# A convolution, attention and expert kernel: a new start of the first image, and a new order where the second attention begins

## The chip, the cores and the metric

The kernel runs on one core of a Trainium2 chip. The metric is the time of one launch on the device in microseconds, the median of several runs. One further execution was recorded by the hardware profiler; its trace gives every instruction with its start, its duration and what it waited for. The engines are TensorE (PE in the profile, with its weight loads as PEld), VectorE (DVE), ScalarE (ACT), GpSimd (POOL) and SyncE (SP), which issues most of the transfers (DMAs). "Granted clock" is the share of TensorE's full clock that the chip's throttle allows.

## The reference

Two images of 256 channels and 56 x 56 pixels pass through two layers, all in float32:

```
x = x + conv_attn(group_norm(x))         # layer 0
t = tokens(x)                            # 6272 tokens of 256 features
t = t + linear_attention(layer_norm(t))  # layer 1
t = t + experts(layer_norm(t))
out = image(t)
```

conv_attn: a 1x1 convolution from 256 to 768 channels, a 3x3 convolution of each channel by itself, and attention of 8 heads over 7 x 7 neighbourhoods. Four heads (split 0) look at direct neighbours, four (split 1) at every second pixel. Scores get a bias from a table by relative position, softmax, the weighted sum of the values, and a projection. group_norm takes mean and variance over groups of 8 channels and all pixels:

```
m = mean(v over 8 channels, h, w);  s = var(...);  (v - m) / sqrt(s + eps)
```

linear_attention: with Q = elu(q) + 1 and K = elu(k) + 1 the sums K'V and K'1 over all tokens of an image, the message Q(K'V) / (Q K'1), a projection, a layer norm, a feed-forward layer of 512 units on token and message, and a second layer norm with weight g2 and bias b2. experts: a router picks the best 2 of 8 experts for each token; each expert is a layer norm, 256 -> 1024, gelu, 1024 -> 256, with bias b2 of its own; the two results are weighed by the softmax of the two logits.

## The kernel before

The program is written in one pass, and a scheduler places each engine's instructions by its own estimate of when their inputs are ready, unless `manual_schedule` keeps the written order of the engines that it names (PE in most of the kernel). `issue_after(x)` puts the instructions of its block behind x on x's engine; `high_priority` moves them forward. Each engine takes its instructions in the order so fixed.

Stages in order of time:

- **First image, 0 to about 430 us.** `Convolutions` loads image 0 into `x_sb` ([128, 2, 3136]: two halves `ct` of 128 channels), and `norm_image` counts it in groups of 448 pixels (`bn_stats`, L478), combines (L480), averages over groups of channels by a product with `g8` (L486, L492), takes the power -1/2 on POOL (L151) and scales `x_sb` in place (L499). `run` then goes over 6 blocks of 128 output channels and over two halves of the image: four groups of rows (8, 8, 8 and 5) get the 1x1 convolution, two products each (L529: one for each ct, each two instructions of PE), ACT copies them into the padded `ypad` (L535), and the 3x3 convolution follows: 8 rows on PE by nine products with diagonal weights (L550), the rest by nine DVE operations (L579) after a first one on ACT (L569). Attention of image 0 is interleaved, its PSUM tiles being `s_ps` (four banks, scores) and `po` (two banks, values and sums). `bias_tables` prepares the tables exp(bias) in the meantime: a frame of zeros `pf` goes to DRAM (L371), the turned biases into it (L374, L379), it comes back (L383), ACT takes the exponential (L387), POOL masks it (L405 to L409), and `fetch` loads the tables `tab` (L714). `wpr` (L639) holds the projection's weights.
- **Linear attention, first half of the tokens, 430 to 747.** Keys (`keys`: statistics, xt L155, K'V L317, running sum L324), then a pipeline over six groups of four token blocks: `queries`, `message`, `feed_forward`, `route`. The remaining convolutions of image 1 fill gaps. b2 is added to the tokens by POOL in `message` (L1925); in the second half and for the block that both halves share it is added in `keys` (L300). `route` has four parts: logits (L2052); the two best (L2084 and the `top_two` chain on DVE); places in the experts' lists (pp, L2099 and L2100, from the partial sums L2095) and `weights` with an exponential on ACT (L2037); and the scatter of the rows into `xs` by POOL (L168), with two stores of the tokens into y2 by ACT (L2000).
- **Second attention, image 1, 747 to 1043.** `Attention.run` is a generator; each of its yields is a step, counted by i. The steps of the first blocks turn 112 x 128 blocks to channels first (`prepare`, `turned`: four transposes on PE, L767; `settle`: copies to qT0, qT1, kT0, kT1 by ACT and DVE, L776 to L792), for which two PSUM banks take turns. A step of scores has four products (L652), the exponential (L656) and the multiply by the table (L657, DVE); a step of values has the products L666. At the steps of `ENDING` the routing of the last two groups of the first half is finished, and from step `LEAD` on every step of scores or values also runs one step of the experts.
- **Experts.** `fetch` loads the 256 rows `xr` of a tile (L1544, behind the scatters) and the expert's weights `w1e` (L1548) and `w2e` (L1552); `turn` transposes xr (L1584), scales it to `xe` (L1587), and `weigh` compares the rows' expert number and makes the weights (`eq` L1572, `idi` L1574, L1575, L1576; DVE); then 8 x 2 products (L1617), gelu (L1621) and 2 x 8 products (L1637) follow. In the second attention, tiles 0 and up run in this way.
- **Linear attention, second half, with experts, 1043 to 1424; experts alone to 1962; output to 1984.**

Of the kernel before, what the change touches and what calls it, by code (L numbers as in the profile page):

```python
# [62 lines left out]
NFI = 14  # L63
LEAD = 22
FILLS = (0, 2, 12, 18, 24, 27, 33)
# [61 lines left out]
def hybrid_kernel(ctx: ExitStack, tc: tile.TileContext, a: dict, out: bass.AP):  # L127
# [139 lines left out]
    def keys(tk, wk, sm, ps, bank, w_k, b2, kx, acc, n0, n, p, first, last, eager):  # L267
# [27 lines left out]
        for k in range(n):  # L295
            nc.scalar.activation(
                t[:, k, :], t[:, k, :], AF.Identity, bias=up[:, 1, k : k + 1], scale=up[:, 0, k : k + 1]
            )
        if b2 is not None:
            nc.gpsimd.tensor_tensor(t, t, b2[p].unsqueeze(1).to_broadcast([rows, n, C]), ALU.add)  # L300
        yield
# [61 lines left out]
    def bias_tables(sp, ac, pp):  # L363

        held = []
        for s in range(2):
            pf = sp.tile([NH * 21, 33], F32, name=f"pf{s}", bufs=1)
            nc.vector.memset(pf, 0.0)
            rpb = a[f"L0_conv_rpb{s}"]
            frame = dram.tile([NH, 21, 33], F32, name=f"frame{s}")  # L370
            nc.sync.dma_start(frame.rearrange("h r c -> (h r) c"), pf)  # L371
            turned = dram.tile([NH * 13, 13], F32, name=f"turned{s}")
            with nc.allow_non_contiguous_dma(reason="676 values"):
                nc.sync.dma_start(  # L374
                    turned, bass.AP(rpb.tensor, rpb.offset + 12, [[13, NH * 13], [-1, 13], [1, 1]])
                )
            held.append((pf, frame, turned))
# [7 lines left out]
        for s in range(2):  # L385
            nw, pf = wide[s], held[s][0]
            nc.scalar.activation(pf, pf, AF.Exp)  # L387
            far = sp.tile([NH * 21, 2], F32, name=f"far{s}", bufs=1)
            nc.sync.dma_start(far, a["c_far"])

# [9 lines left out]
            )  # L400
            nc.sync.dma_start(cm, a[f"c_cm{s}k"].rearrange("p (c j) -> p c j", j=nw))
            o = 0
# [16 lines left out]
    class Convolutions:  # L419


        def __init__(self, ctx):
            pool = lambda name, bufs, **kw: ctx.enter_context(tc.tile_pool(name=name, bufs=bufs, **kw))
            self.xp = pool("p1x", 1, side="right")
            self.cw = pool("p1w", 1, side="right")
            self.yp = pool("p1y", 2, side="right")
            self.sp = pool("p1s", 2, side="right")
            self.banks = [pool("p1pc", 1, space=PSUM, side="right")]
            self.turns = 0
            self.dp = None  # L430

            self.x_sb = self.xp.tile([P, 2, T], F32, name="x_sb")
            self.ypads = [self.cw.tile([P, HH // 2 + 2, WW + 2], F32, name=f"ypad{hf}") for hf in range(2)]
            for hf in range(2):
                nc.gpsimd.memset(self.ypads[hf][:, hf * (HH // 2 + 1), :], 0.0)
                nc.gpsimd.memset(self.ypads[hf][:, :, 0:1], 0.0)
                nc.gpsimd.memset(self.ypads[hf][:, :, WW + 1 : WW + 2], 0.0)
            self.load_x(0)
            self.g8 = self.cw.tile([P, P], F32, name="g8")
            nc.scalar.dma_start(self.g8, a["c_g8"])  # L440
            self.w2 = self.cw.tile([P, 6, 9], F32, name="w2")
            nc.scalar.dma_start(
                self.w2, a["L0_conv_w_qkv2"].rearrange("(oc p) one kh kw -> p oc (one kh kw)", p=P)
            )
            self.wq1 = self.cw.tile([P, 2, 3 * C], F32, name="wq1")
            nc.sync.dma_start(self.wq1, a["w_qkv1_t"].rearrange("(ct p) o -> p ct o", p=P))

# [55 lines left out]

        def run(self):


            w2 = self.w2
            for _ in self.norm_image():
                pass
            yield 0, 0  # L510
            for b, oc in ((b, oc) for b in range(B) for oc in range(6)):
                diag = None
                for hf in range(2):
# [10 lines left out]
                    ypad = self.ypads[hf]  # L524
                    q0 = r0 - hf
                    for g0, n in ((0, 8), (8, 8), (16, 8), (24, 5)):
                        py = self.bank([P, 8, WW], "py")
                        for ct in range(2):
                            nc.tensor.matmul(  # L529
                                py[:, :n, :], self.wq1[:, ct, oc * P : (oc + 1) * P],  # L530
                                self.x_sb[:, ct, (q0 + g0) * WW : (q0 + g0 + n) * WW],
                                start=(ct == 0), stop=(ct == 1),
                            )
                        k0 = 1 - hf + g0
# [72 lines left out]
    class Attention:  # L607
# [6 lines left out]
        def __init__(self, ctx, b, order, banks=None, spare=None):  # L614
# [10 lines left out]
            self.wpr = op.tile([P, 2, C], F32, name="wpr", bufs=1)  # L625
            if not banks:
                self.load_projection()
            self.ones = op.tile([TT, HD], F32, name="ones2", bufs=1)
# [12 lines left out]
        def scores(self, nk, parts, table, nj):  # L641
# [14 lines left out]
            nc.scalar.activation(p[:nk, :, :n], s_ps[:nk, :, :n], AF.Exp)  # L656
            nc.vector.tensor_tensor(grid(p), grid(p), table[:nk], ALU.mult)  # L657
            return grid(p)
# [65 lines left out]
        def run(self):  # L724
# [47 lines left out]
            def settle(g, k, pm):  # L772
# [7 lines left out]
                else:  # L780
                    one = pm[:, :G].rearrange("p (r pi c pj) -> p pi pj r c", pi=2, pj=2, c=28)
                    for pi in range(2):
# [7 lines left out]
                        else:  # L790
                            for pj in range(2):
                                (nc.scalar.copy if banks and g < 2 else evac)(  # L792
                                    kT1[:, pi, pj, :, r0 : r0 + 4, :],
                                    one[:, pi, pj].rearrange("p r (cc c) -> p cc r c", c=KC),
                                )

            def prepare(g):
# [266 lines left out]
    def first_image(conv, ph):  # L1064
# [4 lines left out]
        conv.share(ctx)  # L1069
        run, steps = conv.run(), att.run()  # L1070
        need = next(steps)
        tables = bias_tables(conv.sp, att.pool["ac"], att.pool["p"])
        next(tables)
        for k, (b, done) in enumerate(run):
            if k == 5:
                with tc.issue_after(anchors["copied"]):
                    next(tables, None)
# [277 lines left out]
    class Experts:  # L1355
# [222 lines left out]
        def turn(self, x, pools):  # L1578
# [12 lines left out]
            if x.eq is None:  # L1591
                self.weigh(x)
            b2 = pools.b2e()
# [65 lines left out]
    def linear(ph, tk, half, behind=None):  # L1659
# [258 lines left out]
        def message(n0, n, qz, out):  # L1918
# [3 lines left out]
            for k0 in range(0, n, 2):  # L1922
                if half == 0:
                    tt = tk.at(n0 + k0, 2)
                    nc.gpsimd.tensor_tensor(tt, tt, b2.unsqueeze(1).to_broadcast([P, 2, C]), ALU.add)  # L1925
                pm = ps_h.tile([P, 2, C], F32, name="pm", tag="h")
# [26 lines left out]
        def feed_forward(n0, n, m2T, out):  # L1953
# [15 lines left out]
            for k0 in range(0, n, 2):  # L1969
# [24 lines left out]
                yield  # L1994

        def store(n0, n):

            for k0 in range(0, n, 2):
                kn = min(2, n - k0)
                ins = nc.scalar.dma_start(  # L2000
                    y2[(n0 + k0) * P : (n0 + k0 + kn) * P, :].rearrange("(n p) c -> p n c", p=P),
                    tk.at(n0 + k0, kn),
                )
                if (n0, n) in order[early1:]:
# [28 lines left out]
        def weights(rt, ms, row, n):  # L2033

            r = rt.sm.tile([P, 4], F32, name="rsum")[:, :n]
            with tc.issue_after(newest[3]) if half and newest[3] is not None else nullcontext():
                nc.scalar.activation(ms[1], ms[1], AF.Exp)  # L2037
# [95 lines left out]
        def all_keys():  # L2133
# [6 lines left out]
            for i in range(len(pairs) + 2):  # L2140
                for k in (1, 0, 2):
                    j = i - k
                    if j == i and j < len(pairs):
                        live[j] = keys(
                            tk, wk, sm, ps_a, bank, w_k, b2 if half or pairs[j][1] == 1 else None, kx, acc, *pairs[j], j == 0, j == len(pairs) - 1, j < 3 and half == 0
                        )
# [327 lines left out]
```

## Time and profile before

| | |
|---|---|
| median of three runs | 1997.98 us (1995.13 to 2001.15) |
| profiled execution | 1985.54 us, its span 1983.8 us |
| PE busy | 1840.1 us (93%) |
| DVE, ACT, POOL busy | 1093.3, 705.8, 578.8 us |
| first product of the 1x1 convolution | 18.49 us from the start |
| mean granted clock | 0.972; 0.51 from 750 to 775, 0.67 from 775 to 800 |

A row of a timeline is: start, duration, engine, line, operation, output<-inputs, shape, count, and in brackets how long the engine stood idle before it and what ended that. "ACTq" and "SPq" are the queues of those engines issuing a DMA. A stretch's row gives the busy time of each engine with the number of instructions in brackets, the granted clock, the DMA engines' share and GB/s.

### The profile page before, as it was taken

To read this page: it belongs to the slowest core of one execution; us is meant where nothing else is said; L and a number is where in the kernel's file an instruction comes from. 1 tells how busy PE (TensorE), PEld (TensorE's weight loads), DVE (VectorE), ACT (ScalarE), POOL (GpSimd) and SP (SyncE) were. 2 spreads that over 40 slices of the span, in tenths; PEclk is the share of its full clock that TensorE was granted. 3 is DMA by queue.
4 is the path that set the end of the run, shared out by engine and by line. 5 is a ranking of instruction groups with operands and counts; after the bars stand their busy time and mean duration, and the time that the engine had idled before them with its cause. 6 is when DMAs were issued, how large, how long until landed. Compare 5 with 4: busy or idle time off the path is not lost.

```text
span 1983.8 us, 27692 instructions
## 1 busy us (share of the span) xinstructions
PE 1840.1 (93%) x9996; PEld 1304.7 (66%) x9996; DVE 1093.3 (55%) x2728; ACT 705.8 (36%) x1337; POOL 578.8 (29%) x634
## 2 busy tenths in 40 slices
PE   6999899988989997999989989999999999999996
PEld 3444454556645564665668755668788888888885
DVE  6887988889888546555557434655622222222121
ACT  2233324334434223544536543323322222222332
POOL 4520042025202444111126311345422323222221
PEclk9999999999989996999999999999999999999998
DMA  4644422350003334754464210114677676767995
GB/s 113 152 114 128 152 75 84 101 151 35 25 33 94 107 85 140 205 153 137 130 191 126 72 35 32 46 62 133 182 227 198 185 201 186 200 190 197 299 279 166
DMA packets 200147, 268.79 MB, mean 135 GB/s; under 512 B 30952, under 2 KB 158614, under 8 KB 199760
## 3 DMA queue, kind: packets, MB, share of 16 engines
q1 hardware_dynamic: 167920, 223.95, 37.4%
q0 software_dynamic: 19728, 27.54, 7.4%
q10 hardware_dynamic: 12352, 15.43, 2.3%
q8 instruction: 81, 1.33, 0.3%
q14 instruction: 66, 0.54, 0.1%
HBM read 200.19 MB, written 70.95 MB: 137 GB/s over the span
## 4 chain that ended last, share of the span: by engine, by line
PE 48%; DMA 5%; DVE 3%; ACT 3%; issue 1%; SPq 0%; POOL 0%; ACTq 0%; DVEq 0%; POOLq 0%
PE ph L1617 13%; PE py L1637 13%; PE p L1961 4%; DMA xr<-xs 2%; PE x L1637 2%; PE py L1977 2%; PE x L1617 2%; DMA xs<-in_c_fill 2%; PE po L666 2%; PE pm L1931 1%; PE kx L317 1%; PE x L359 1%; PE kp L305 1%; PE pq L1888 1%; PE px L1584 1%; PE s_ps L652 1%
## 5 line engine op out<-in xcount | busy, mean ns | idle before, releaser
L1617 PE MATMUL ph<-xe,w1e 128*128 128x256 f32 (+1 forms) x1448 | 309.2, 369 | 10.6 <-ACT hT L1621 4.1
L1637 PE MATMUL py<-w2e,hT 128*128 128x256 f32 x1392 | 311.3, 379 | 0.0
L1621 ACT ACTIVATE hT<-ph,sv 128x256 f32<-128x256 f32 (+1 forms) x362 | 165.7, 462 | 387.3 <-PE ph L1617 384.2
L1617 PEld LDWEIGHTS ph<-xe,w1e 128*128 128x128 f32 x1448 | 261.2, 190 | 49.8 <-ACT hT L1621 6.1
L1637 PEld LDWEIGHTS py<-w2e,hT 128*128 128x128 f32 x1392 | 260.1, 190 | 33.1 <-issue 0.2
L168 POOL DMA_INDIRECT y<-yt,idi x101 | 160.2, 1587 | 322.6 <-DVE yt L1643 178.2
L579 DVE SCALAR_TENSOR_TENSOR yc<-ypad,w,yc 128x1120 f32<-128x1120 f32 x144 | 202.5, 1410 | 31.4 <-ACT yc L569 29.0
L262 POOL TENSOR_TENSOR rs<-rs,mhalf 128x2 f32<-128x2 f32 (+3 forms) x90 | 72.8, 812 | 325.4 <-DVE rs L261 277.6
L529 PE MATMUL py<-x_sb,wq 128*128 128x448 f32 (+1 forms) x384 | 155.9, 538 | 8.3 <-ACT ypad L535 4.4
L656 ACT ACTIVATE p<-s_ps 112x952 f32<-112x952 f32 (+5 forms) x88 | 102.1, 1160 | 150.6 <-PE s_ps L652 101.4
L1574 DVE CAST idi<-xr 128x2 int32<-128x2 f32 (+1 forms) x53 | 10.9, 205 | 255.9 <-DMA xr<-xs 255.9
L657 DVE TENSOR_TENSOR p<-p,tab 112x952 f32<-112x952 f32 (+5 forms) x88 | 122.0, 1389 | 47.4 <-ACT p L656 47.3
L550 PE MATMUL pc<-ypad,diag 128*128 128x448 f32 x324 | 131.4, 547 | 0.0
L1643 DVE SCALAR_TENSOR_TENSOR yt<-py,eq,yt 128x256 f32<-128x256 f32 x87 | 41.7, 482 | 156.3 <-PE py L1637 156.1
L1599 POOL TENSOR_SCALAR yt<-b2e,eq 128x256 f32<-128x256 f32 x101 | 50.7, 507 | 257.6 <-DMA b2e<-in_L_ffn_b 198.6
L529 PEld LDWEIGHTS py<-x_sb,wq 128*128 128x128 f32 x384 | 72.2, 199 | 71.4 <-issue 55.7
L168 POOL DMA_INDIRECT xs<-row,si x98 | 97.5, 995 | 64.4 <-DVE si L2108 34.7
L572 DVE SCALAR_TENSOR_TENSOR yc<-ypad,w,yc 128x784 f32<-128x784 f32 x96 | 104.9, 1114 | 1.3 <-ACT yc L569 0.9
L666 PE MATMUL po<-p,v 98*32 98x170 f32 (+5 forms) x960 | 70.8, 376 | 28.6 <-DVE p L657 15.3
L550 PEld LDWEIGHTS pc<-ypad,diag 128*128 128x128 f32 x324 | 60.0, 191 | 52.3 <-issue 48.5
L1961 PE MATMUL p<-xT,fw 128*128 128x512 f32 (+1 forms) x208 | 93.6, 573 | 0.0
L1961 PE MATMUL p<-m2T,fw 128*128 128x512 f32 (+2 forms) x224 | 93.4, 539 | 0.0
(394 smaller groups left out, 2883.8 us busy)
## 6 DMA issues: line engine op xcount, KB each, us to landing
w1e<-in_L_ffn_W SPq DMA_DIRECT2D x53, 1024.0 KB
w2e<-in_L_ffn_W SPq DMA_DIRECT2D x53, 1024.0 KB
yd<-yc SPq DMA_DIRECT2D x24, 784.0 KB
ld<-yd SPq DMA_DIRECT2D x28, 448.0 KB
xr<-xs SPq DMA_DIRECT2D x48, 260.0 KB
b2e<-in_L_ffn_b SPq DMA_DIRECT2D x53, 128.0 KB
t<-td SPq DMA_DIRECT2D x12, 512.0 KB
y<-t ACTq DMA_DIRECT2D x24, 256.0 KB
```

The costliest lines, as they stand in the source:

```text
L168: ins = nc.gpsimd.indirect_dma_start(out=dst[:, :], out_offset=bass.IndirectOffsetOnAxis(ap=index, axis=0), in_=src, in_offset=None, **kw,)
L529: nc.tensor.matmul(py[:, :n, :], self.wq1[:, ct, oc * P : (oc + 1) * P], self.x_sb[:, ct, (q0 + g0) * WW : (q0 + g0 + n) * WW], start=(ct ...
L550: nc.tensor.matmul(pc, diag[:, tap, :], ypad[:, dy : dy + SHARE, dx : dx + WW], start=(tap == 0), stop=(tap == 8),)
L572: nc.vector.scalar_tensor_tensor(yc[:, y0:y1, :], src, w, yc[:, y0:y1, :], ALU.mult, ALU.add)
L579: nc.vector.scalar_tensor_tensor(yc[:, y0:y1, :], src, w, yc[:, y0:y1, :], ALU.mult, ALU.add)
L656: nc.scalar.activation(p[:nk, :, :n], s_ps[:nk, :, :n], AF.Exp)
L657: nc.vector.tensor_tensor(grid(p), grid(p), table[:nk], ALU.mult)
L666: nc.tensor.matmul(dst[hs] if w is None else den[hs], v[:nk, hs] if w is None else w[:nk, :], p[:, h, :, o : o + q.shape[2]], start=first ...
L1617: nc.tensor.matmul(p1, x.w1[:, ct, j * P : (j + 1) * P], x.xe[:, ct, :], start=(ct == 0), stop=(ct == 1),)
L1621: newest[3] = nc.scalar.activation(hT[:, j, :], p1, AF.Gelu, bias=x.sv[:, 4 + j : 5 + j]).ins
L1637: nc.tensor.matmul(py, hT[:, j, h * P : (h + 1) * P], x.w2[:, j, :], start=(j == 0), stop=(j == NJ - 1),)
L1961: nc.tensor.matmul(p1[:, :w], fw1[:, k, oc * P : (oc + 1) * P], rhs, start=(k == 0), stop=(k == 3))
```

## The change

1. **Head.** The loads of x go half by half over both queues, with g8 and the first 128 columns of the weights between; a new `first_block`, with PE and DVE in the written order, counts and scales half 0 while half 1 loads, and starts six row groups' products with half 0. The six places are the attention's s_ps and po banks; half 1's products complete them, and `run` takes them from `self.ready`. The clearing of pf, the small loads of `bias_tables` and image 0's wpr are put behind DVE's second count of half 1 or behind the first frame's store.
2. **b2.** It is always added in `keys`; the addition in `message` is gone.
3. **Stores and exponentials.** The exponentials in `weights` and the token stores that are written after the first block's last copy (`settled`) are put behind that copy on ACT. This concerns the last two groups of the first half.
4. **Rows compared.** `weigh`, called from `turn`, is put behind the latest multiply by a table on DVE.
5. **Experts two steps later.** LEAD is 24 instead of 22.

```diff
-LEAD = 22
+LEAD = 24
@@ keys
-        if b2 is not None:
-            nc.gpsimd.tensor_tensor(t, t, b2[p]..., ALU.add)
+        nc.gpsimd.tensor_tensor(t, t, b2[p]..., ALU.add)
@@ message
-                if half == 0:
-                    tt = tk.at(n0 + k0, 2)
-                    nc.gpsimd.tensor_tensor(tt, tt, b2..., ALU.add)
@@ bias_tables
-            nc.vector.memset(pf, 0.0)
+            with tc.issue_after(anchors["counted"]), tc.high_priority():
+                nc.vector.memset(pf, 0.0)
...
-            nc.sync.dma_start(frame.rearrange("h r c -> (h r) c"), pf)
+            ld = nc.sync.dma_start(frame.rearrange("h r c -> (h r) c"), pf)
+            anchors.setdefault("framed", ld.ins)
# the loads of turned, far and cm, and image 0's load_projection():
+            with tc.issue_after(anchors["framed"]), ...
@@ Convolutions
-            self.load_x(0)
+            for ct in range(2):
+                for k, (c0, c1) in enumerate(zip((0, G, 3 * G, 5 * G), (G, 3 * G, 5 * G, T))):
+                    eng = nc.scalar if k % 2 else nc.sync
+                    eng.dma_start(self.x_sb[:, ct, c0:c1], xv[0, :, ct, c0:c1])
+                if ct == 0:
+                    nc.scalar.dma_start(self.g8, a["c_g8"])
+                    nc.sync.dma_start(self.wq1[:, :, :P], wq1[:, :, :P])
...
-            nc.sync.dma_start(self.wq1, a["w_qkv1_t"]...)
+            nc.scalar.dma_start(self.wq1[:, :, P:], wq1[:, :, P:])
@@ first_block (new; count, mean, variance, scaled and products are small helpers)
+            with tc.manual_schedule(engines={PE, DVE}):
+                count(0, *range(NG))
+                mean(0)
+                variance(0)
+                count(1, 0)
+                scaled(0, 0, G)
+                products(0, 0)
+                count(1, 1)
+                scaled(0, G, T // 2)
+                products(0, 1)
+                count(1, *range(2, NG))
+                mean(1)
+                scaled(0, T // 2, T)
+                products(0, 2)
+                variance(1)
+                products(0, 3, 4, 5)
+                scaled(1, 0, G)
+                products(1, 0)
+                scaled(1, G, T // 2)
+                products(1, 1, 2)
+                scaled(1, T // 2, T)
+                products(1, 3, 4, 5)
+            self.ready = {r[:2]: d for r, d in zip(rows, places)}
@@ Convolutions.run
+                        py = self.ready.pop((hf, g0), None)
+                        if py is None:
+                            py = self.bank([P, 8, WW], "py")
+                            for ct in range(2):
+                                self.product(py, oc, hf, g0, n, ct)
@@ scores
-            nc.vector.tensor_tensor(grid(p), grid(p), table[:nk], ALU.mult)
+            anchors["scaled"] = nc.vector.tensor_tensor(...).ins
@@ settle, k == 3
+                                if banks and g == 0:
+                                    anchors["settled"] = ins.ins
@@ Experts.turn
-                self.weigh(x)
+                with tc.issue_after(anchors["scaled"]):
+                    self.weigh(x)
@@ linear
+        def behind():
+            turned = run == 0 and half == 0 and "settled" in anchors
+            return tc.issue_after(anchors["settled"]) if turned else nullcontext()
# in store: with behind(): the DMA; in weights, first half: with behind(): the exponential
```

## The prediction

> **What bounds the kernel now.** First the page's head, then the chain of waits, then busy time by stretches, and last the timelines of single engines where TensorE (PE) stands still. Engine shares and granted clock by fortieths of the span (49.6 us each):
>
> ```profile
> PE 1840.1 (93%) x9996; PEld 1304.7 (66%) x9996; DVE 1093.3 (55%) x2728; ACT 705.8 (36%) x1337; POOL 578.8 (29%) x634
> PE   6999899988989997999989989999999999999996
> PEclk9999999999989996999999999999999999999998
> ```
>
> PE is the bound almost everywhere; two places stand out: the first slice (6) and the sixteenth (7), where the clock falls too (6); the last is the output. The stretches around that seam (columns: PE, weight loads, DVE, ACT, POOL, then clock, DMA share, GB/s):
>
> ```profile
> 750.00:775.00 25.00, 21.20 (x140) 13.56 (x140) 18.14 (x100) 9.86 (x26) 12.82 (x13) 0.51 0.43 124
> 775.00:800.00 25.00, 17.28 (x126) 9.59 (x123) 13.20 (x42) 7.63 (x12) 9.55 (x12) 0.67 0.70 239
> ```
>
> PE works at half clock there. After 800 nearly all such stretches have 22 to 25 us of PE and a clock of 1.00, to the end; so time saved at the seam is handed on. The chain of waits names the transfers at the seam:
>
> ```profile
> 781.09 2.48 DMA xs<-row,si
> 783.58 2.76 DMA xr<-xs
> 788.51 2.14 PE po L666 x16
> 793.54 3.78 PE x L1617 x8
> ```
>
> The last scatter of routed rows lands at 783.57, the first expert's rows (xr) at 786.34; until then PE has no expert work. But why does an attention product, po, start only at 788.51? The PE and DVE timelines answer:
>
> ```profile
> 788.51 1.16 PE L666 MATMUL po<-p,v 112*32 112x280 f32 x8 [6.77 <-DVE p L657]
> 790.54 1.12 PE L1584 MATMUL x<-ident,xr 128*128 128x128 f32 x4
> 793.54 3.78 PE L1617 MATMUL x<-xe,w1e 128*128 128x256 f32 x8 [0.81 <-DVE xe L1587]
> ```
>
> ```profile
> 786.37 0.23 DVE L1572 TENSOR_SCALAR eq<-xr,etmA 128x2 f32<-128x2 f32 x1 [5.72 <-DMA xr<-xs]
> 787.14 1.32 DVE L657 TENSOR_TENSOR p<-p,tab 112x1120 f32<-112x1120 f32 x1
> ```
>
> The comparison eq needs xr. It was queued ahead of the multiply that PE waits for, so DVE stood still 5.72 us and PE 6.77. A smaller stall lies earlier:
>
> ```profile
> 750.04 0.37 ACTq L2000 DMA_DIRECT2D y<-t  x1
> 750.70 0.20 ACT L2037 ACTIVATE m<-m 128x4 f32<-128x4 f32 x1 [3.99 <-DVE m L2096]
> 750.81 0.53 ACT L776 ACTIVATE qT<-x 128x448 f32<-128x448 f32 x1
> ```
>
> ACT waited with a store and an exponential for DVE while the transposed block lay ready from 747.6; PE, short of a PSUM bank, idled 3.76 us to 751.39. At the start, rows of DVE, then of PE:
>
> ```profile
> 14.28 0.53 DVE L480 BATCH_NORM_AGGREGATE mv<-st 128x2 f32<-128x42 f32 x2
> 17.92 1.71 DVE L499 TENSOR_SCALAR x_sb<-x_sb,gm,rs_gn 128x448 f32<-128x448 f32 x3 [0.85 <-POOL rs_gn L151]
> ```
>
> ```profile
> 18.49 1.11 PE L529 MATMUL py<-x_sb,wq 128*128 128x448 f32 x1 [1.62 <-DVE x_sb L499]
> ```
>
> No product runs before the whole image is loaded (11.63), counted (14.8) and given a scale (17.9).
>
> **What the Trainium skill says.** "TensorE: Matmul & The Clock Gate", Part 1: the array is at half rate until about 3.4 us of sustained work. The trace agrees: the first 448-column instructions leave 0.75 us apart, later ones 0.375, and the clock record turns full at 23.4, half from 750.4 to 777.7, and half again from 784.6 to 798.2. "Perfetto Trace Analysis", Tensor Engine Instruction: ACT, DVE and GpSimd are strict FIFO; the eq row above is that. "GPSIMD Engine Reference", Specifications: its SBUF interfaces are shared with VectorE. The trace shows three DVE operations of 128x2 to 128x4, usually 0.16, at 1.21 to 1.23 us each while POOL's three b2 additions run (435.8 to 439.5).
>
> **Part by part.**
>
> *The head.* Channel half ct 0 now loads first, over both queues. Landings went 896 KB per 2.2 us; half 0 then lands near 7.9, g8 and the first 128 weight columns near 8.2, half 1 near 11.7. DVE counts seven groups at 0.575 and trails the last landing by two: 9.15. Aggregation 0.27; from there to the scale took 3.1 us (14.8 to 17.9): 12.5. First scaling 0.4, so PE starts at 13.0 against 18.49. Counting half 1 interleaves: 17.2, aggregate 17.5, PE's mean product waits for it (idle some 1.5 us), scale at 21.1, half 1 scaled by 23.6. PE's six row groups of ct 1 then run 22.2 to 26.4 if the clock is full, to some 28 if it is half. Before, four groups were done at 26.6. Two groups more are 2 groups x 2 halves x 2 instructions of 0.375 = 3.0 us of PE. So the head gains 3.2 at best, 1.6 at half clock; I take 2.0. The convolution's DVE chain (28.41 before) begins about 1.9 earlier.
> What is moved with it: the cleared frames go behind DVE's second count of half 1 (13.5), so the frame stores leave SP near 14 instead of 9.45 and 11.71, and the tiny "turned" loads, far, masks and wpr behind the first of them. The "turned" loads took from 9.89 to 24.7 and 12.11 to 32.0, most of it behind 2.5 MB of image and weights, so I expect 0 to 3 us later. Behind them on ACT sits the exponential of pf at 39.18, and behind that copies that PE needs: a cost of 0 to 2, I take 0.5. wpr is first used at 184: cover enough. The rest of the weights is needed for the second output block, near 45. Net: 1.5 gained.
>
> *b2 in the keys.* Twelve POOL additions of 1.27 us leave the message code. But their row (L1925) shows them at 435.8 to 500.3, already in the keys stage, as fillers. Count and place stay; only their rank rises. Value 0, bounds -3 and +15 (rival below).
>
> *Stores and exponentials behind the first turns.* ACT then copies at 747.7, and the turns of the first block end near 749.9. Next in PE's hand-written order is pp (L2099, L2100), which reads DVE's third partial sum (L2095), done at 752.91; it started at 753.02. The wait is replaced almost whole: gain 0 to 1, I take 0. The two groups' four stores (0.37 of ACT each) move from 723 to 750 to about 751 to 752; they land 2.1 us later, and the twelve table loads that wait on SP for them (0.83 each) then end near 763 instead of 756.6. Their readers are at 777.4 and 803.9; the next SP load left at 765.8. Cost 0.
>
> *Rows compared behind a multiply, and two steps later.* With eq no longer ahead, the multiply runs about 781.0 to 782.35, and po at 782.4 to 783.7. Two transposed copies and the next exponential (1.1) follow, scores at 784.1, the second multiply to 785.7, po to 787.1: two steps of attention that stood behind the expert's turn now stand ahead of it and cover xr's landing. The turn runs 787.1 to 787.8, the next band's scores (0.84) to 788.6. w1e lands at 790.17 as before (it is issued after xr), so PE waits 1.6 there, and the first eight expert matmuls take 2.0 at full clock: 792.2. The same work, with those scores, was done before at 798.8 + 0.8 = 799.6. **Gain 7.4.** Bounds: 3.5 if the clock halves again, 11 if the scatter chain comes earlier as well. Late next: w1e. The fetch moves two steps on SP past the next band's wpr and v loads: v, before held back by wpr until 795.4, comes earlier; the second xr (796.2 before) comes some 1 us later, its turn was at 808.4. Two expert steps leave the attention and follow under linear attention's second half: PE work kept, 0.
>
> *Comparison behind the multiply in the other turns.* DVE waits 18.5 us in six idi casts for xr; PE gaps beside them are 0.7 to 1.3. I take 0.5, bounds 0 and 2.
>
> Sum: 1.5 + 7.4 + 0.5 = 9.4, say 9. The profiled execution took 1985.5 (span 1983.8); it would take 1976.5. The runs' median is 1998.0, 12.5 above it, with no row to explain that; I carry the difference over: **1989.0**.
>
> **Rivals.**
> *Same (17%).* The clock halves again at 784 as it did, since PE still has four small gaps there (0.65, 0.3, 1.0, 1.6), and the head gives nothing because the pf exponential blocks ACT. 3.5 + 0.5 = 4: 1994. For it: 27 us at half clock with PE 85% busy. Against: from 781.2 to 784.6, the 3.4 us before the clock fell, PE would be busy 72% instead of 17%.
> *Faster still (15%).* PE keeps full clock from 750 on, because the first turns run early, and DVE's sums come earlier: the scatter chain gains 3, po and turns 2 more: 14, 1984. Against it: pp's wait stays.
> *Slower (12%).* The b2 additions, now of the keys' own rank, enter POOL's FIFO ahead of the power that DVE waits for, in a stretch with DVE at 72.9 of 80 us: 12 x 1.27 = 15.2 lost, less 9: 2004. It decides once DVE's wait for the power (0.5 us in all before) exceeds some 0.8 per pair. For it: the 5.27 us PE gap at 435 lies beside three such additions. Against: in the second half, which already has that order, DVE waits only 2.1 us for POOL.
> That the changes in order do nothing is unlikely: the edges are fixed, not hints.
>
> **How the numbers follow.** The forecast's own case has 56% and spans -5 to -13. About 0.3% (6 us) is what a measurement of this kernel can tell from no change; 52 of the 56 lie beyond it. Faster by more: 0.52 + 0.15 = 0.67; within: 0.04 + 0.17 = 0.21; slower: 0.12. The range from 1980 to 2001 takes in the forecast's own case and the same, and parts of the two others; it leaves out about 2 in 10.
>
> **What would show it.** Right: no PE gap over 2 us between 775 and 800 and eq behind a multiply; first product near 13; pp still waiting for DVE; L1925 gone and L300 with twelve more, in the same stretch; PE gap at 435 about as before. Wrong: 430 to 510 longer by over 5 us; the expert's turn waiting for xr over 2 us; pf's exponential preceded by ACT idle of over 2 us.

## The result, and the profile after

The changed kernel takes **1993.05 us** at the median of 20 runs (1984.83 to 1998.57), the kernel before 1997.44 in 20 runs beside them (1990.70 to 2004.94). The ratio is **0.9975, 95% interval 0.9965 to 0.9984**: 4 to 5 us less, about half of the 9 forecast. The profiled execution of the changed kernel took 1991.22 us (span 1989.3), 5.7 more than that of the kernel before, which had been quicker than any of its 20 runs. The two spans can't be subtracted; the stages are compared below with more profiles.

The head of the page after, in the order of before (line numbers, here and below, are those of each kernel's own file): totals, PE by fortieths of the span, granted clock.

```profile
PE 1840.3 (93%) x10000; PEld 1305.1 (66%) x10000; DVE 1092.3 (55%) x2733; ACT 703.4 (35%) x1335; POOL 573.7 (29%) x635
...
PE   6899899987999996999989989999999999999996
...
PEclk9999899999999995999999999999999999999998
```

PE's work is the same to 0.2 us. The first slice is 6 as before, and the seam's, the sixteenth, is a digit lower than before, in busy share (6 for 7) and in clock (5 for 6). The two stretches there (PE, weight loads, DVE, ACT, POOL, clock, DMA share, GB/s):

```profile
750.00:775.00 25.00, 18.78 (x127) 11.11 (x127) 14.66 (x71) 7.79 (x18) 10.69 (x10) 0.50 0.88 185
775.00:800.00 25.00, 18.58 (x180) 10.28 (x172) 17.31 (x49) 9.87 (x14) 10.58 (x12) 0.78 0.84 275
```

The DMA share in the first rose from 0.43 to 0.88 and the granted clock is half throughout, in one piece from 745.2 to 786.2 where it had come in two. PE's timeline after at the seam, every row behind an idle time of over 1.2 us that leads to the expert's first products, and those:

```profile
746.57 0.64 PE L2186 MATMUL x<-chosen,tri 128*128 128x32 f32 x2 [2.39 <-ACT kT L870]
750.48 1.01 PE L845 MATMUL x<-ident,ld 112*128 112x112 f32 x4 [2.10 <-DVE slot L2189]
763.73 1.01 PE L845 MATMUL x<-ident,ld 112*128 112x112 f32 x4 [2.26 <-ACT qT L854]
777.30 0.63 PE L845 MATMUL x<-ident,ld 112*128 112x112 f32 x2 [1.78 <-DMA ld<-yd]
780.19 0.64 PE L845 MATMUL x<-ident,ld 112*128 112x112 f32 x2 [2.25 <-issue]
791.80 0.68 PE L744 MATMUL po<-p,v 112*32 112x280 f32 x8 [1.53 <-issue]
792.88 0.66 PE L1667 MATMUL x<-ident,xr 128*128 128x128 f32 x4
794.24 1.99 PE L1701 MATMUL x<-xe,w1e 128*128 128x256 f32 x8
```

The stalls of 3.76 and 6.77 us have gone; six smaller ones stand in their place. DVE's comparison now finds its rows landed and waits for nothing:

```profile
792.67 0.22 DVE L1655 TENSOR_SCALAR eq<-xr,etmA 128x2 f32<-128x2 f32 x1
```

### The profile page after: what moved, and what is told of

It is laid out like the page before. It is cut to its first block, busy times and chain, and to the rows that moved or that the text cites. A ratio compares the mean times of both kernels' runs of the same rounds, so it can differ in the third digit from the quotient of the medians.

```text
span 1989.3 us, 27714 instructions
## 1 busy us (share of the span) xinstructions
PE 1840.3 (93%) x10000; PEld 1305.1 (66%) x10000; DVE 1092.3 (55%) x2733; ACT 703.4 (35%) x1335; POOL 573.7 (29%) x635
## 3 DMA queue, kind: packets, MB, share of 16 engines
q8 instruction: 81, 1.33, 0.3%
## 4 chain that ended last, share of the span: by engine, by line
PE 68%; DVE 14%; DMA 5%; ACT 4%; issue 4%; POOL 2%; SPq 1%; ACTq 0%; POOLq 0%; DVEq 0%
PE py L1721 14%; PE ph L1701 14%; PE p L2042 7%; PE po L744 4%; DVE yc L659 4%; PE py L583 3%; PE pc L630 3%; PE py L2058 3%; PE x L1721 3%; DVE yc L652 2%; PE s_ps L730 2%; PE x L1701 2%; PE pq L1972 2%; PE pm L2012 2%; PE x L358 1%
## 5 line engine op out<-in xcount | busy, mean ns | idle before, releaser
L1701 PE MATMUL ph<-xe,w1e 128*128 128x256 f32 (+1 forms) x1464 | 315.2, 371 | 9.7 <-ACT hT L1705 7.2
L1701 PEld LDWEIGHTS ph<-xe,w1e 128*128 128x128 f32 x1464 | 266.6, 192 | 47.4 <-ACT hT L1705 8.7
L583 PE MATMUL py<-x_sb,wq 128*128 128x448 f32 (+1 forms) x360 | 143.8, 530 | 7.7 <-ACT ypad L615 4.3
L583 PEld LDWEIGHTS py<-x_sb,wq 128*128 128x128 f32 x360 | 65.9, 194 | 67.0 <-issue 49.9
```

What stands on the lines that cost most here:

```text
L583: nc.tensor.matmul(py[:, :n, :], self.wq1[:, ct, oc * P : (oc + 1) * P], self.x_sb[:, ct, q0 * WW : (q0 + n) * WW], start=(ct == 0), stop= ...
L1701: nc.tensor.matmul(p1, x.w1[:, ct, j * P : (j + 1) * P], x.xe[:, ct, :], start=(ct == 0), stop=(ct == 1),)
```

## The experiments

Twelve kernels ran. Kernels measured together share the runs of the kernel before, whose median differed from group to group (1997, 1992, 1985, 1985 us), so only ratios are compared. One thousandth is 2 us. "Eq behind" says whether the comparison of `weigh` stands behind the multiply on DVE; "b2, stores as before" that these two parts of the change are left out.

| kernel | head | eq behind | experts at step | other | ratio to before (95%) |
|---|---|---|---|---|---|
| changed | new | yes | 24 | | 0.9975 (0.9965 to 0.9984) |
| head_only | new | no | 22 | b2, stores as before | 1.0008 (0.9997 to 1.0019) |
| eq_only | old | yes | 22 | b2, stores as before | 0.9963 (0.9949 to 0.9977) |
| lead24_only | old | no | 24 | b2, stores as before | 0.9981 (0.9970 to 0.9993) |
| seam_only | old | yes | 24 | b2, stores as before | 0.9982 (0.9969 to 0.9995) |
| lead22 | new | yes | 22 | | 0.9958 (0.9947 to 0.9969) |
| lead22_nosettled | new | yes | 22 | stores as before | 0.9956 (0.9940 to 0.9972) |
| keysteps | new | yes | 24 | two steps taken up in the keys | 0.9969 (0.9955 to 0.9983) |
| mn_dve | new | yes | 24 | mn on DVE in the second half | 0.9955 (0.9944 to 0.9966) |
| eq_mn | old | yes | 22 | the same; b2, stores as before | 0.9960 (0.9945 to 0.9976) |
| head_order | reordered | yes | 22 | | 0.9972 (0.9963 to 0.9982) |
| head_four | four groups | yes | 22 | | 0.9968 (0.9955 to 0.9980) |
| before_again | old | no | 22 | a second profile of before | 1989.70 us, one run |

The profiles behind it, in stretches (us). "Attention" runs from the last product into the tile pp in the first half of linear attention (L2084 in before, done at 742.6; the routing's last products come after it) to the second attention's last scores. It is divided where the ninth product of the first expert with w1e starts (798.78 in before): what lies ahead has the first turn, what follows the others. "Late" runs from the last key product of linear attention's second half to the end. Experts two steps later take about 4 us of PE (two rows like the 1.99 at 794.24) out of the attention and put them behind it.

| | before | before again | eq_only | lead22 | lead24_only | seam_only | changed | keysteps | mn_dve |
|---|---|---|---|---|---|---|---|---|---|
| attention, first turn | 56.2 | 56.1 | 53.0 | 59.4 | 58.1 | 61.0 | 60.2 | 65.0 | 59.5 |
| attention, other turns | 205.5 | 212.5 | 204.4 | 204.4 | 196.0 | 196.0 | 196.1 | 196.0 | 196.4 |
| attention, whole | 261.7 | 268.6 | 257.5 | 263.8 | 254.1 | 257.1 | 256.3 | 261.0 | 255.8 |
| late | 863.7 | 862.8 | 866.9 | 868.4 | 870.7 | 875.0 | 879.4 | 868.2 | 864.8 |

The last three kernels differ only behind the attention, and still their first row spreads over 5.5 us: a smaller difference in that row, from one profile each, shows little. The second row is far steadier; between steps 22 and 24 neither can be compared, since at 24 two more steps of attention lie ahead of the division.

**Where the gain is: more at the fourth turn than at the first.** The edit in `eq_only` and `lead24_only`:

```diff
# eq_only
+            anchors["scaled"] = nc.vector.tensor_tensor(grid(p), grid(p), table[:nk], ALU.mult).ins
-                self.weigh(x)
+                with tc.issue_after(anchors["scaled"]):
+                    self.weigh(x)
# lead24_only
-LEAD = 22
+LEAD = 24
```

> The kernel before with one edit: the comparison eq and its casts come behind the attention's last multiply; experts start at step 22 as before, and the old head stays. Theory C (this edit carries the change's gain: with the casts in front, DVE and behind it PE stood still for rows not yet landed at three turns of experts beside the attention, up to 9.67 us of DVE in the run with the head alone): ratio to before 0.9955 (0.994 to 0.997), some 8 to 10 us less, and no DVE wait for rows over 1 us between 780 and 900. Theory D (as the prediction had it, 0.5 us for the turns after the first, and the first turn on PE still waits for its rows): 2 to 3 us less, ratio 0.9985 to 0.999.

> The kernel before, unchanged, for a second profile. Theory C: the first profile was a lucky one; this one takes some 1992 and shows a PE gap of 4 to 7 us near 827, where DVE's cast waits for the fourth turn's rows, as with the head alone. Theory D: the gaps of the first profile again, 1.3 us at 830, and the longer time spread evenly.

The second profile of before shows a stall that the first had only in small (4.59 us of DVE, 1.33 of PE at 830). DVE's row, then PE's:

```profile
832.58 0.17 DVE L1574 CAST idi<-xr 128x2 int32<-128x2 f32 x1 [9.40 <-DMA xr<-xs]
```

```profile
834.62 1.02 PE L666 MATMUL po<-p,v 112*32 112x238 f32 x8 [6.14 <-issue]
```

The fourth tile's cast stands in DVE's queue ahead of an attention multiply, and its rows land at 832.5; PE, whose product needs that multiply and starts 2 us after DVE's release, stands still for 6.14. The head alone shows it too (9.67 us of DVE, 6.40 of PE). In `eq_only` no expert's turn up to 900 makes DVE wait for rows; from 775 to 1045 the casts' waits (us in total, times, longest) fell from 23.5 to 1.6:

```profile
DVE idi L1574 <- DMA xr<-xs: 23.5, 6, 9.4
```

```profile
DVE idi L1574 <- DMA xr<-xs: 1.6, 1, 1.6
```

and it is 7 us faster, 0.9963. Theory C holds. The row of the other turns says the same: with eq behind and experts at step 22 it is 204.4 in five kernels of six (206.2 in `lead22_nosettled`), and with eq in front 205.5, 212.5 and, in `head_only`, 212.9. How often the long stall comes can't be told from three profiles; the second one of before, at 1989.70, is 4.5 above the median of the runs beside it, so it isn't typical either.

At the first turn, for which the prediction had counted the whole gain, most of the waiting stayed: PE's transposes wait in place of the multiply, and then the weights' product waits too.

```profile
772.64 0.68 PE L666 MATMUL po<-p,v 112*32 112x280 f32 x8 [0.63 <-DVE p L657]
...
777.75 1.09 PE L1584 MATMUL x<-ident,xr 128*128 128x128 f32 x4 [3.97 <-DMA xr<-xs]
...
782.34 3.75 PE L1618 MATMUL x<-xe,w1e 128*128 128x256 f32 x8 [2.42 <-DVE eq L1575]
...
787.44 1.99 PE L1618 MATMUL x<-xe,w1e 128*128 128x256 f32 x8
```

0.63 + 3.97 + 2.42 = 7.0 us, for 6.77 + 0.81 = 7.6 before. But po now runs ahead of the wait, and the row at 787.44 comes 53.0 us after the last pp, and 53.7 in `eq_mn`, for 56.2 and 56.1 in the two profiles of before. So some 2.5 to 3 us of the 7 seem to come from here; by the spread of that row this isn't shown.

> The kernel before with the experts two attention steps later (LEAD 24) and nothing else: it completes the square with eq alone (0.9963), both (0.9982) and neither (1). Theory G (two steps later costs 3 to 4 us in linear attention's second half and gains nothing at the seam once eq is behind the multiply; with eq in front it still takes the first stall of 6.7 us away, but not the one of the fourth turn): ratio 0.998 to 1.000. If the two edits were simply additive: 1.0019. If two steps later were the gain: 0.9965.

0.9981, inside theory G's range, but with its parts the other way round. The first stall stays:

```profile
782.26 1.16 PE L666 MATMUL po<-p,v 112*32 112x280 f32 x8 [6.35 <-DVE p L657]
```

and the fourth turn's goes: the casts still wait 24.0 us in all, but between 800 and 905 PE has no gap over 1.2 us, so the waiting no longer reaches it. The other turns take 196.0 us with eq in front as with eq behind (`seam_only`). So the two edits cure the same stall, and together (`seam_only`, 0.9982) they bring no more than the later steps alone. They don't add: the sum would have been 0.9944.

> The kernel before with two edits alone: eq behind the multiply, and experts two steps later. Theory A: the gap of 6.77 us at 781.7 goes, linear attention's second half gives about 8 back: 1995 to 1999, ratio 0.999 to 1.001, with PE stalls of 3 us or more between 1310 and 1410. Theory B: the gain stays whole, 1990, ratio 0.9965, and no such stalls.

The second attention took 257.1 us, 4.6 less than the quick profile of before and 11.5 less than the other; `eq_only`, with two expert steps more in it, 257.5. The late stretch took 875.0. Both of theory A's statements, the PE stalls of over 3 us (3.52 at 1329 and 3.19 at 1364) and some of the gain given back, are seen, though PE still stood 5.05 us at 780; the ratio lies between A and B.

**What two steps later cost.** At step 24 against step 22 the ratio is higher by 0.0017 with the new head (changed against `lead22`) and by 0.0019 with the old one (`seam_only` against `eq_only`). Weighted together: 0.0018 plus or minus 0.0012, or 3.5 us. (The two kernels with other heads below, also at step 22, came out at 0.9972 and 0.9968. If their heads cost nothing, the four at step 22 with new heads average 0.9965, and the two steps cost some 2.5 us, plus or minus 1.9.)

> The changed kernel with the experts starting two attention steps earlier, as before (LEAD 22); eq still comes behind a multiply. Theory A: the stalls near 1326 and 1361 go (8 us back), but the first expert's turn again stands ahead of two attention products on PE and waits for the rows to land, a PE gap of 4 to 5 us near 782: 1993 - 8 + 5 = 1990. Theory B: nothing is won back late, and the seam loses 5: 1998.

0.9958: some 3.4 us under the changed kernel, theory A's sum though not its parts. The stall at 1326 went but one of 3.14 at 1347 came, and the gap near 782 is 2.15 and not 4 to 5. The changed kernel's two stalls on PE:

```profile
1329.73 2.08 PE L1972 MATMUL pq<-xT_ab,w_q 128*128 128x128 f32 x8 [3.51 <-ACT hT L1705]
...
1364.84 3.78 PE L1701 MATMUL ph<-xe,w1e 128*128 128x256 f32 x8 [4.13 <-ACT hT L1705]
```

and ACT ahead of the second:

```profile
1362.30 0.37 ACTq L2087 DMA_DIRECT2D y<-t  x1
1363.95 0.47 ACT L2022 ACTIVATE mn<-pm,rs 128x256 f32<-128x256 f32 x1 [6.30 <-POOL rs L262]
1364.32 0.83 ACT L1705 ACTIVATE hT<-ph,sv 128x256 f32<-128x256 f32 x2
```

PE waits for what the expert's gelu (hT) releases, a bank of PSUM. The gelu stands in ACT's queue behind a store and behind mn, the scaling of a message, which waits for POOL's power. In before PE had products of w2 at that place, whose gelus were long done. Two tests of that.

> The changed kernel, with the two expert steps that now leave the attention taken up again in the keys of linear attention's second half (at i = 5 and 8), so that from its queries on every expert step stands where it stood in the kernel before. Theory A (the seam's gain is kept, but two steps later the experts' gelus fall behind ACT work that waits, in linear attention's second half): the PE stalls of 3.51 us at 1326 and 4.13 us at 1361 go, PE is back above 96 of 100 us between 1310 and 1410 at clock 1.00, and the time falls by 8 (5 to 12) below the changed kernel's 1993: 1985, ratio to before 0.994. Theory B (those stalls come from another part of the change, the b2 additions or the stores, or differ from run to run): they stay or move, time 1991 to 1995, ratio 0.997 to 0.999.

```diff
-                    if i < 3 or i % 3 == 1:
+                    if i < 3 or i % 3 == 1 or i in (5, 8):
```

Half a miss: the stall at 1326 went, one of 3.15 us at 1348 came in its place, and PE was busy 94.2 us of the 100 from 1310 to 1410 (90.6 in the changed kernel, 96.8 before). 0.9969 can't be told from 0.9975. So the place of the steps matters, but putting them back doesn't settle the cause. The next edit leaves the order as it is and takes the wait out of the gelu's queue:

```diff
-                    nc.scalar.mul(mn[:, k, :], pm[:, k, :], rs[:, k : k + 1])
+                    if half:
+                        nc.vector.tensor_scalar(mn[:, k, :], pm[:, k, :], rs[:, k : k + 1], None, ALU.mult)
+                    else:
+                        nc.scalar.mul(mn[:, k, :], pm[:, k, :], rs[:, k : k + 1])
```

> The changed kernel (LEAD 24) with one edit: in linear attention's second half the messages are scaled (mn) on DVE instead of ACT, so that no expert's gelu stands behind a scaling that waits for POOL's power. Theory A (that wait is what two steps later costs): the PE stalls of 3.5 us near 1326 and 4.1 us near 1361 go and the ratio falls from 0.9975 to 0.9955. Rival (the store's wait or the order of PE's own work is the cost): the stalls stay, or others take their place, 0.997 to 0.998.

0.9955, as theory A had it: 0.0020 (plus or minus 0.0014) below the changed kernel, as much as the two steps cost. The stall at 1361 is gone, that at 1326 is 1.78 us. The stretch 1310 to 1375 in the changed kernel, then in this one (columns as above):

```profile
1310.00:1375.00 65.00, 57.35 (x269) 46.87 (x262) 31.43 (x170) 20.64 (x52) 25.07 (x28) 0.89 0.30 90
```

```profile
1310.00:1375.00 65.00, 63.22 (x322) 52.24 (x321) 35.98 (x185) 23.09 (x57) 29.04 (x32) 1.00 0.37 112
```

PE is busy 5.9 us more, and its clock stays full where it had fallen to half twice (6.8 us each, from 1328.9 and 1363.1, shortly before each stall ended).

> The kernel before with eq behind the multiply (LEAD 22, old head, 0.9963 alone) and the messages of linear attention's second half scaled on DVE. With LEAD 22 ACT's scalings wait some 3 us for the power: Theory A gives 0.996 to 0.9965, hardly better than eq alone. Rival (the gelus behind the scalings cost in every order): 0.995.

0.9960 against 0.9963: with experts at step 22 there is nothing to win there, as expected. The cost belongs to the later steps, not to mn in every order.

**The head.**

> The kernel before with the new head alone. Forecast for this part: 1.5 less (0 to 3): 1996, ratio 0.9992. Rival (all that the change gave is the head, since the changed kernel's profile is some 4 us ahead by the end of the first attention): 4 less, ratio 0.998.

1.0008: no gain, and the rival of 4 us is out. PE starts at 13.65, near the forecast, yet DVE's convolution chain starts later than with the old head: at 29.9 to 31.2 us in six profiles with the new one, 27.4 to 28.8 in six with the old one (means 30.4 and 28.3). Rows of the changed kernel, PE and then ACT, which copies the products to where DVE reads them:

```profile
14.63 3.36 PE L583 MATMUL s_ps<-x_sb,wq 128*128 128x448 f32 x4 [1.95 <-DVE x_sb L549]
...
24.96 2.93 PE L583 MATMUL s_ps<-x_sb,wq 128*128 128x448 f32 x8
```

```profile
27.93 1.70 ACT L615 COPY ypad<-s_ps 128x448 f32<-128x448 f32 x4 [17.45 <-PE s_ps L583]
29.49 0.58 ACT L615 COPY ypad<-po 128x448 f32<-128x448 f32 x1
29.91 1.27 ACT L649 ACTIVATE yc<-ypad,w 128x1120 f32<-128x1120 f32 x1
```

With the old head (`seam_only`) ACT copied each group as it came, from 21.72 on, and yc began at 27.53. Here four groups lie in one tile, s_ps; ACT's first copy starts as the last of the four ends (24.96 + 2.93 = 27.89), then come four copies in a row and the fifth group's, 2.0 us to yc. And 3.2 us of PE's earlier start, from 21.97, went into products that aren't needed yet: half 0 of groups five and six.

> The changed kernel with experts at step 22 and one more edit in the head: on PE the ct 0 products of the fifth and sixth row group come behind the ct 1 products of the first four, instead of ahead of them. Theory E (the head gained nothing because those products, 3 us at half clock, hold up the first half image, and ACT copies the first group only when all four in its PSUM tile are done): ACT's first copy comes at 24.5 instead of 26.5, DVE's convolution chain starts at 27.5 to 28 instead of 29.9, and the time falls by 0 to 2 us against step 22 alone: ratio 0.9955. Theory F (the scaling of ct 1 on DVE is what is late): the chain starts at 29.5 to 30, ratio 0.9958.

> The changed kernel with experts at step 22 and a head whose hand-written part makes only the first four row groups; groups five and six are made in the loop as before. Theory E2 (DVE's convolution chain starts late because ACT's copies, in order, wait for six groups' products instead of four): ACT's copies come at 24.5 to 26.5, DVE's chain starts at 27.5 to 28.2 instead of 29.9, the time falls by 0 to 2 us from 0.9958: 0.995 to 0.996. Rival F (scaling of ct 1 on DVE and half clock are what is late): the chain starts at 29 or later, 0.9958.

Both missed. In `head_order` the four copies come at 26.41 (`lead22`: 26.57), but ACT's queue holds the fifth group's copy ahead of yc, and that group is now later: yc at 29.85, DVE at 31.11. In `head_four` the first copy comes at 26.52, because PE has a product of the loop (two instructions, 1.70 us at half clock) in the slot that was freed; DVE starts at 29.82. The times (0.9972 and 0.9968, intervals that overlap that of `lead22`) don't speak for either. What all three show is that the copies wait for the whole of s_ps; which of the two, the shared tile or the second half's scaling on DVE (done at 24.4 in the changed kernel), would have to move first to gain anything wasn't separated.

**Stores and exponentials.**

> The changed kernel with experts at step 22 and the stores and exponentials of linear attention's first half left in their old order ahead of the turns' copies. If that part is worth nothing, as forecast: ratio 0.9958 as with it, the turns' gap of 4 to 5 us at 744 back, and the last scatter still landing 48 us after the last pp of the routing. If it carries part of the gain: slower by 2 us or more, 0.9970.

0.9956 here and 0.9958 in `lead22`: worth nothing either way that can be told (plus or minus 4 us), and the stall of 3.76 at 745 is back, as expected.

## Why the prediction was right or wrong

The sign and the range hold: 1993.05 measured, 1989.0 forecast, 1980 to 2001. A quarter of a per cent is inside the 0.3% that the text had put as the edge of no change, though its interval leaves out zero. The sum was 9.4 and about 4.5 came; that is not one term short but errors of both signs, and most of the gain in another place. That the range held is in part luck: the errors happened to offset each other.

- **Bound.** Right: PE, with the seam as the place where it stands still. What the prediction could not see is that its one profile of before was a quick one, 12.5 us under the median "with no row to explain that". The second profile has a row for part of it: 6.14 us at the fourth turn, 4.8 more than in the first.
- **Head, 1.5.** Wrong: 0 (1.6 slower, between 0.6 faster and 3.8 slower). First product right (14.63, and 13.65 to 14.35 in the others, for 13.0). The step that failed is "The convolution's DVE chain (28.41 before) begins about 1.9 earlier": it began 2.1 later. The prediction compared six groups done at 26.4 with four done at 26.6 and took products for the thing that is waited for; DVE waits for ACT's copies, and those wait for a tile. The exponential of pf (0.5) cost nothing: ACT reached it at 39.07 without idle, for 39.18 before.
- **b2, 0.** Nothing speaks against it, though no run had this part alone. Head, b2 and stores together gave 1.2 us less (plus or minus 2.4; changed against `seam_only`, `lead22` against `eq_only`). The additions stay fillers of the same stretch, in the same pattern, as the changed kernel's first row of POOL shows beside PE's gap there (5.27 before):

```profile
432.40 3.71 POOL L299 TENSOR_TENSOR t<-t,b 128x512 f32<-128x512 f32 x3
```

```profile
436.92 3.78 PE L304 MATMUL kp<-w_k,xT 128*128 128x256 f32 x8 [5.33 <-DVE xT L185]
```

  The keys from the first product to the last took 79.2 us, in before 78.3 and, again, 79.8. The slower rival is out.
- **Stores and exponentials, 0.** The sum is right as far as the runs can tell, its working is not. The wait was replaced as said (2.39 and 2.10 for 3.76). But the table loads on SP ended near 772 instead of 763 (among them SP issued nothing for 8.2 us from 752.70, and the trace doesn't name what it waited for), and the attention's own blocks (ld) behind those left at 772.62 for 765.81 before. PE waited for them: 1.78 us above, and up to 9.86 in `head_four`; what ended the 2.25 above isn't named. The prediction priced the readers of the tables and not the loads queued behind them. In time it cost nothing that can be told; that the chain of scatters ends later anyway is argued, not shown.
- **Eq and two steps later at the first turn, 7.4.** The mechanism in DVE's queue was right, the place wrong. The time from the last pp to the end of the first eight expert products, with the same attention work done, was 57.0 us in both profiles of before (to 799.6 in the first, as the prediction counts) and 58.9 in the changed kernel: there the first turn gained nothing. The step that failed is "the multiply runs about 781.0 to 782.35, and po at 782.4 to 783.7": that po came at 788.12 and the turn at 792.88 for 787.1, though this profile had reached the last pp 5.3 us earlier than before's. The attention that stands ahead of it was late, in part for the ld blocks of the last point. Without the stores' part, `seam_only` still held PE from 780.13 to 785.19: DVE, ACT and PE went on within 1.0 us of the last scatter's landing (784.20), and the trace doesn't name what released them. Why the attention stops for the scatters is open.
- **Other turns, 0.5 (0 to 2).** Mis-sized: most of the gain was here. Eq alone gave 7.4 us (4.6 to 10.1, from 0.9963); by the table, the other turns took 1.0 less than in the first profile of before and 8.0 less than in the second, and the first turn perhaps 3. The prediction had read 18.5 us of waiting in six casts and set it against PE gaps of 0.7 to 1.3 in a profile in which the worst of them happened to be small.
- **"Two expert steps leave the attention and follow under linear attention's second half: PE work kept, 0."** Mis-sized: 3.5 us lost (plus or minus 2.3), since with eq behind the multiply the later steps have nothing left to cure (2.5 by the wider count above). PE's work was kept; its order against ACT's queue was not.

Eq -7.4, two steps +3.5, head, b2 and stores near 0: -4, as measured. The change with experts at step 22, or at step 24 with mn on DVE, is better than both kernels: 0.9955 to 0.9958, another 3.5 to 4 us under the changed one. Which of these is best can't be told within their intervals.

## What to carry to other kernels

An instruction that waits for a transfer holds up its whole queue, so look at each such wait with the question of what stands behind it, and take a second profile before setting its price: a wait can be 4.6 us in one execution and 9.4 in the next. Two cures for the same stall don't add, and moving work of one engine "for nothing" changes whom it meets in the queues of the others: here a gelu behind a scaling that waited for a power. Starting products earlier helps only if what empties them, and what that is queued behind, starts earlier too.

## What the runs showed that was not expected

- A stall can cost more than its length, but how much more isn't fixed by it. In otherwise full work those of 3.51 and 4.13 us in the changed kernel brought 6.8 us of half clock each, as did one of 3.52 in `seam_only`; one of 3.50 in `lead24_only` brought 3.4, and that of 3.19 in `seam_only` none. "TensorE: Matmul & The Clock Gate", Part 1, of the Trainium skill gives a free-running window of about 3.4 us. The traces agree: in all fourteen, each of the 199 stretches at half clock within the kernel is a multiple of 3.41 us.
- At the seam the clock stayed at half for 41 us, from 745.2 to 786.2 in the changed kernel, with PE busy 75% from 750 to 775 and no idle time over 2.4 us.
- ACT's first copy out of a PSUM tile of four banks began as the fourth bank's product ended, in each of the three heads: 27.93 after 27.89 in the changed kernel, 26.41 after 26.38 in `head_order`, 26.52 after 26.49 in `head_four`. Whether the chip or the program's own waits ask for that wasn't tested.
